# Attention and mixture-of-experts block: the products with v are given out later and in longer runs, and three small steps change place

## The chip, the cores and the metric

The kernel runs on one core of one Trainium2 chip. The metric is the device time of one execution in microseconds (us). Before the change it is 630.76 us, the median of three runs (628.73 to 631.48). Five engines work side by side, each on its own list of instructions in order: TensorE (PE, with its weight loads shown as PEld), VectorE (DVE), ScalarE (ACT), GpSimd (POOL) and SyncE (SP), which here only issues DMAs. They wait for one another through semaphores.

## The reference, cut to what matters

The input x has 8 batches of 512 tokens with 128 features. All is float32.

```python
x = x + attention(layernorm(x), Wq, Wk, Wv, Wo, bo)      # 16 heads of 8, causal
x = x + moe(layernorm(x), gate_w, w1, b1, w2, b2)        # 8 experts, the best 2 of each token

# attention, for every batch and head
s = (q * 8**-0.5) @ k.T;  s = where(causal, s, -inf)
o = softmax(s) @ v;       out = concat(o) @ Wo + bo
# experts, for every token
probs = softmax(x @ gate_w.T);  p, idx = top_k(probs, 2)
y = sum(p[j] * (relu(x @ w1[idx[j]] + b1[idx[j]]) @ w2[idx[j]] + b2[idx[j]]) for j in (0, 1))
```

## The kernel before

The work is written as seven generators (`setup`, `project`, `shifts`, `attend`, `route`, `experts`, `sums`). Each yields a planned time, in units of one batch, before each step. A loop at the end of the file (L1246) always goes on with the generator whose planned time is the least, so these numbers fix the order of the instructions on PE, ACT, DVE and SP; POOL follows its own dependences. Nothing else sorts the work: a step that yields a later number stands later in every one of these lists.

`project` normalises a batch, makes q, k and v, sends q and k through DRAM and loads them back in the layout that the score products need (L393). `shifts` makes the scores once, in `s` tiles, only to find each row's maximum (DVE `tensor_reduce`, L509); the negative maxima become two more rows of q (L463). `attend` makes the scores a second time, transposed (`st`, L644), so that ACT can turn them into exponentials (L650) in a tile `pt`, and POOL then sets to zero what lies above the diagonal (L656). Last come the products with v (L574): `va` holds v with a column of ones, and the four heads of a group write four strips of 32 partitions of one PSUM tile `po`, each product as two instructions in the profile.

A batch has four groups of four heads. The causal scores of a group come in three units (`T_UNITS`): unit 0 is key block 0 with 512 columns, unit 1 is key blocks 1 and 3 with 384 and 128 columns, unit 2 is key block 2 with 256 columns. Each unit has two steps, one for each pair of heads; after each step `go_on` (L552) is called. It gives out one waiting run of products, if there is one, and one waiting later step. A run of products is queued at the end of its unit, so it stands on PE one step after the scores that it needs. After unit 2 ACT copies `po` out (`ob`, L582), and three later steps follow: `divide` (transposes `oqp`, L592, then division on DVE), `out_T` and `out_project`. The `s` and `st` tiles share four PSUM banks (`ps_sc`); `pt` has six buffers; `po` has one.

`route` finds the experts, and 100-odd lines of small DVE operations give every token its slot; `scatter` (POOL, L913) writes the tokens to their slots in DRAM (`xs`). `dispatch` gives out tiles of 128 slots to experts. In its last part for the first seven batches, eight values are loaded into SP's registers (L892), and eight DMAs clear the rest of each expert's last tile (L900). `experts` then works tile by tile: SP loads the expert's row of `wrows` (w1, b1 and b2 side by side, L996) and gathers four tiles of tokens at a time (L1073); PE multiplies by w1 (`ph`, L1143), ACT or DVE applies bias and relu (L1150, L1152), PE multiplies by w2 (`py`, L1007), DVE adds b2 (`yo`, L1011), and `store` scatters the rows to `ys` (L1042). The row numbers for that (`to`, made by three to five small DVE operations from L1024 to L1041) are made inside `store`, at the first tile of four. From slice to slice expert tiles stand between the attention steps: steps 0 to 2 of `STEPS` (40 tiles) start during attention, 38 tiles come after it. `sums` adds the weighted outputs at the end (L1221).

`setup` fills `wrows` during the first batches. It writes all of b1 by one DMA (L260) and all of b2 by one (L263), and then w1, w2 and the cleared parts of `xs` in 28 pieces, 0.085 apart (L284).

Of the kernel before, what the change touches and what calls it, by code (L numbers as in the profile page):

```python
# [9 lines left out]
F32 = mybir.dt.float32  # L10
I32 = mybir.dt.int32
BF16 = mybir.dt.bfloat16
AF = mybir.ActivationFunctionType
ALU = mybir.AluOpType
# [10 lines left out]
def preln_attn_moe(ctx: ExitStack, tc: tile.TileContext, x, wq, wk, wv, wo, bo,  # L25
# [195 lines left out]
    def setup():  # L221
        yield -0.95
        packed_buffers(1)
        yield -0.5

        nc.gpsimd.memset(lower_bf, 1.0)
        nc.gpsimd.affine_select(
            out=lower_bf, in_=lower_bf, pattern=[[1, P]], compare_op=ALU.is_gt,
            fill=0.0, base=0, channel_multiplier=-1,
        )  # L230
        nc.gpsimd.iota(
            number, pattern=[[1, MAXT], [0, E]], base=0, channel_multiplier=0,
            allow_small_or_imprecise_dtypes=True,
        )
        for k in range(2):
            nc.gpsimd.iota(
                room[k], pattern=[[ROOM[k], E + 1]], base=0, channel_multiplier=0,
                allow_small_or_imprecise_dtypes=True,
            )

        for t, by_tile, by_row in ((place_no, P, 1), (token, 1, NT)):
            nc.gpsimd.iota(
                t, pattern=[[by_tile, t.shape[1]]], base=0, channel_multiplier=by_row,
                allow_small_or_imprecise_dtypes=True,
            )
        for e in range(E):
            nc.gpsimd.memset(rev[:, :, e : e + 1], float(E - e))
        gw_raw = const.tile([E, D], F32, tag="gwraw", name="gw_raw")
        nc.sync.dma_start(out=gw_raw, in_=gate_w)
        b1_raw = const.tile([E * FC, P], F32, tag="b1raw", name="b1_raw")  # L250
        nc.sync.dma_start(out=b1_raw, in_=b1.rearrange("e (c f) -> (e c) f", f=P))
        yield 0.4
        for dst, src, n in ((gwT, gw_raw, E), (b1T, b1_raw, E * FC)):
            pt = mm_tile(f"setup_{dst.name}")
            nc.tensor.transpose(pt[:, :n], src, ident[:n, :n])
            nc.vector.tensor_copy(
                dst if n == E else dst.rearrange("p e c -> p (e c)"), pt[:, :n]
            )
        yield 0.5
        nc.sync.dma_start(  # L260
            out=wrows[:, :, F : F + FC].rearrange("e p c -> p e c"), in_=b1T
        )
        nc.sync.dma_start(  # L263
            out=wrows[:, :, F + FC :], in_=b2.unsqueeze(1).to_broadcast([E, P, D])
        )

        pieces, after = [], []
        for e in range(E):
            after.append((wrows[e, :, 0:F], w1[e]))
            after.append((  # L270
                w2_sb.rearrange("p (c e h) -> p c e h", c=FC, e=E)[:, :, e],
                w2[e].rearrange("(c p) h -> p c h", p=P),
            ))
        for k, c0 in ((0, E * ROOM[0] // P), (1, 0)):
            n = xs[k].shape[0] // P
            for c in range(c0, n, 4):
                m = min(4, n - c)
                pieces.append((
                    xs[k].rearrange("(c p) d -> p c d", p=P)[:, c : c + m],
                    empty.unsqueeze(1).to_broadcast([P, m, XROW]),  # L280
                ))
        for n, (dst, src) in enumerate(pieces[:2] + after + pieces[2:]):
            yield 0.6 + 0.085 * n
            nc.sync.dma_start(out=dst, in_=src)  # L284


# [256 lines left out]
        indirect[0] = ins  # L543

    def attend():
        products, late, on = [], [], {}


        po = ps_o.tile([P, T], F32, tag="po", name="po")
# [2 lines left out]
        def go_on():  # L552
            ready = late[:1]
            del late[:1]
            if products:
                products.pop(0)()
            for step in ready:
                step()

# [1 line left out]
            v = u if len(unit) == 2 else 0  # L561
            return pt[:, v, at : at + W]

        def product(b, g, pts, unit, first, last):
            va = va_buf[b % 2]
            for j in sorted({j for bank in unit for _, j, _ in bank}):
                W = T - j * P
                for pr in range(2):
                    for bank in unit:
                        for u, i, at in bank:  # L570
                            if i != j:
                                continue
                            h = 2 * pr + u
                            nc.tensor.matmul(  # L574
                                po[32 * h : 32 * h + VC, j * P :],
                                lhsT=va[:, j, HG * g + h, :],
                                rhs=at_cols(pts[pr], unit, u, at, W),
                                start=(first and j == 0), stop=(last and j == 2),
                            )
            if last:  # L580
                ob = work.tile([P, T], F32, tag="ob", name=f"ob_{b}_{g}", bufs=1)
                nc.scalar.copy(ob, po)  # L582
                late.append(lambda: divide(b, ob, g))
                if g == G - 1:
                    added.add(b)
# [40 lines left out]
        for b in range(B):  # L626
            for g in range(G):
                yield b + g / G
                assert (b, g, 2) in shifted
                q2, k2 = q2_buf[b % 2], k2_buf[b % 2]  # L630
                for i, unit in enumerate(T_UNITS):
                    pts = []
                    for pr in range(2):
                        yield b + g / G + (2 * i + pr + 0.5) / 24
                        n = 2 * g + pr
                        pt = work.tile(
                            [P, 2, T], F32, tag="pt", name=f"pt_{b}_{n}_{i}", bufs=6
                        )
                        for v, bank in enumerate(unit):
                            ps = ps_sc.tile(  # L640
# [19 lines left out]
                            )  # L660
                        pts.append(pt)
                        go_on()
                    products.append(lambda b=b, g=g, pts=pts, unit=unit, i=i: product(
                        b, g, pts, unit, i == 0, i == 2))
                attended.add((b, g))
        t = B
        while products or late:
# [141 lines left out]
    def dispatch(s, soon):  # L809
# [76 lines left out]
        if k == 0 and last:  # L886

            fill = small.tile([1, E], I32, tag="fill", name=f"fill_{s}", bufs=1)
            V.tensor_tensor(fill, pc[0:1, :E], room[k][0:1, :E], ALU.add)
            yield soon()  # L890
            found = [
                nc.values_load(  # L892
                    fill[0:1, e : e + 1], engines=[mybir.EngineType.SP],
# [50 lines left out]
    def experts():  # L944
# [69 lines left out]

        sent = {k: [] for k in range(len(GROUPS))}

        def store(s, i):
            k, b, _, last = STEPS[s]
            first, m = quad(s, i)
            if i == first:  # L1020

                x = xg[s, first]
                other = small.tile([P, 4], F32, tag="other", name=f"other_{s}_{i}")
                V.tensor_tensor(  # L1024
                    other[:, :m], x[:, :m, D], slot_no[s][:, first : first + m],
                    ALU.not_equal,
                )
                goal = small.tile([P, 4], F32, tag="goal", name=f"goal_{s}_{i}")
                V.scalar_tensor_tensor(  # L1029
                    goal[:, :m], other[:, :m], float(NTOK), x[:, :m, D + 1],  # L1030
                    ALU.mult, ALU.add,
                )
                if last:
                    gap = small.tile([P, 4], F32, tag="gap", name=f"gap_{s}_{i}")
                    V.scalar_tensor_tensor(
                        gap[:, :m], x[:, :m, D], 0.0, place_no[:, first : first + m],
                        ALU.is_lt, ALU.mult,
                    )
                    V.tensor_tensor(goal[:, :m], goal[:, :m], gap[:, :m], ALU.add)  # L1039
                to[s, first] = small.tile([P, 4], I32, tag="to", name=f"to_{s}_{i}", bufs=3)  # L1040
                V.tensor_copy(to[s, first][:, :m], goal[:, :m])  # L1041
            ins = nc.gpsimd.indirect_dma_start(  # L1042
                out=ys[k],
                out_offset=bass.IndirectOffsetOnAxis(
                    ap=to[s, first][:, i - first : i - first + 1], axis=0
                ),
                in_=yo[s, first][:, i - first, :], in_offset=None,
            )
            in_order(ins)
            for other in sent[k]:  # L1050
                tc.declare_no_dep(
                    ins.ins, other, reason="every slot has its own row, or one nobody reads"
                )
            sent[k].append(ins.ins)
            if last and i == STEPS[s][2] - 1:
                tiled[k] = sent[k]
# [65 lines left out]
        def turns():  # L1122
            for s, i in quads:
                yield when(s, i + 1) - min(0.05, 1.3 * TILES_AT[s][1])
                turned[s, i] = transposed(s, i)

        yield when(0, 0)
        fetch_to(3)
# [3 lines left out]
        for n, (s, i) in enumerate(tiles):  # L1132
            first, m = quad(s, i)
            yield when(s, i + 1)
            if after(s, i):
                ph = ps_sc.tile([P, T], F32, tag="sc", name=f"ph_{s}_{i}")
                hT = work.tile([P, 2, T], F32, tag="pt", name=f"hT_{s}_{i}", bufs=6)
                hT = hT[:, 0, :].rearrange("p (c t) -> p c t", c=FC)
            else:
                ph = mm_tile(f"ph_{s}_{i}")  # L1140
# [139 lines left out]
```

## Time and profile before

| | |
|---|---|
| median of the runs | 630.76 us |
| profiled execution: its own time | 627.79 us |
| profiled execution: its span, first to last instruction | 626.0 us |
| PE busy | 555.2 us, 89% |
| DVE busy | 435.0 us, 69% |
| ACT busy | 305.3 us |
| POOL busy | 286.1 us |
| mean granted TensorE clock | 0.955 |
| products with v (L574) | 1024 instructions, 107.1 us busy |
| scores for the maximum (L486) and second scores (L644) | 117.1 and 107.4 us |

All of this is from one execution, taken by the hardware profiler. A row of the groups gives the line in the kernel, the engine, the operation, what is written and read, how often, and then the busy time, the mean of one and the idle time of the engine before it. The ends of matmuls are modelled; their starts are measured. So the cost of a run of products is read here as the time from its first start to the start of the next PE instruction. Starts and windows are in us from the first instruction.

### The profile page before, as it was taken

To read this page: it belongs to the slowest core of one execution; us is meant where nothing else is said; L and a number is where in the kernel's file an instruction comes from. 1 tells how busy PE (TensorE), PEld (TensorE's weight loads), DVE (VectorE), ACT (ScalarE), POOL (GpSimd) and SP (SyncE) were. 2 spreads that over 40 slices of the span, in tenths; PEclk is the share of its full clock that TensorE was granted. 3 is DMA by queue.
4 is the path that set the end of the run, shared out by engine and by line. 5 is a ranking of instruction groups with operands and counts; after the bars stand their busy time and mean duration, and the time that the engine had idled before them with its cause. 6 is when DMAs were issued, how large, how long until landed. Compare 5 with 4: busy or idle time off the path is not lost. (4 is left out here: it accounts for less than half of the span.)

```text
span 626.0 us, 13451 instructions
## 1 busy us (share of the span) xinstructions
PE 555.2 (89%) x4356; PEld 361.9 (58%) x4356; DVE 435.0 (69%) x1410; ACT 305.3 (49%) x679; POOL 286.1 (46%) x468
## 2 busy tenths in 40 slices
PE   8799299999989999998989999899989698999980
PEld 6544144544544554555554666566646568999980
DVE  4476366889889888686978786579785225633584
ACT  3135056566546656454654655355545344455530
POOL 3123033434636544473564355635733553676441
PEclk9889689999999999998998999899998899999995
DMA  2714816825863742470265236522321468888783
GB/s 74 179 44 119 161 25 170 201 71 157 210 110 111 170 125 89 100 175 26 81 146 127 66 120 152 151 74 65 94 70 52 121 208 258 228 269 254 245 288 98
DMA packets 66713, 85.83 MB, mean 137 GB/s; under 512 B 10652, under 2 KB 49732, under 8 KB 65636
## 3 DMA queue, kind: packets, MB, share of 16 engines
q1 hardware_dynamic: 61252, 74.90, 45.4%
q0 software_dynamic: 4544, 9.38, 4.6%
q10 hardware_dynamic: 848, 0.69, 0.4%
q8 instruction: 36, 0.59, 0.4%
q14 instruction: 33, 0.27, 0.1%
HBM read 61.14 MB, written 26.09 MB: 139 GB/s over the span
## 5 line engine op out<-in xcount | busy, mean ns | idle before, releaser
L509 DVE TENSOR_REDUCE pm<-s 128x1 f32<-128x512 f32 (+2 forms) x320 | 206.9, 682 | 69.0 <-PE s L496 68.9
L650 ACT ACTIVATE pt<-st 128x512 f32<-128x512 f32 x320 | 178.0, 599 | 105.2 <-PE st L644 96.5
L656 POOL TENSOR_SCALAR_AFFINE_SELECT pt<-pt 128x256 f32<-128x256 f32 x256 | 102.0, 411 | 208.5 <-ACT pt L650 200.6
L486 PE MATMUL s<-k,q 72*128 72x512 bf16 (+3 forms) x512 | 117.1, 308 | 20.1 <-DMA k<-kparts 13.9
L644 PE MATMUL st<-q,k 74*128 74x384 bf16 (+3 forms) x512 | 107.4, 306 | 4.0 <-DVE pm L509 2.1
L574 PE MATMUL po<-pt,va 128*9 128x512 f32 (+3 forms) x1024 | 107.1, 448 | 3.4 <-POOL pt L656 3.3
L1042 POOL DMA_INDIRECT ys<-yo,to x78 | 75.8, 972 | 54.7 <-DVE x L1221 13.1
L486 PEld LDWEIGHTS <-q 72*128 72x128 bf16 x512 | 46.9, 100 | 75.8 <-issue 60.2
L1007 PE MATMUL py<-w_sb,hT 128*128 x624 | 85.0, 279 | 2.3 <-ACT hT L1150 0.9
L496 PE MATMUL s<-mask_bf,ident_bf 128*128 128x256 bf16 (+1 forms) x320 | 82.4, 257 | 0.0
L1007 PEld LDWEIGHTS py<-w_sb,hT 128*128 128x128 f32 x624 | 76.8, 193 | 6.6 <-issue 2.5
L913 POOL DMA_INDIRECT xs<-xn_f,slot x64 | 62.8, 981 | 15.6 <-issue 13.2
L644 PEld LDWEIGHTS <-k 74*128 74x128 bf16 x512 | 46.0, 101 | 27.1 <-issue 13.6
L574 PEld LDWEIGHTS po<-pt,va 128*9 128x9 f32 x1024 | 23.7, 90 | 60.2 <-issue 31.8
L1143 PE MATMUL ph<-xgT,wt 128*128 128x128 f32 x288 | 42.6, 294 | 6.9 <-DMA wt<-wrows 6.9
L1143 PEld LDWEIGHTS ph<-xgT,wt 128*128 128x128 f32 x288 | 37.4, 203 | 11.8 <-issue 6.2
L496 PEld LDWEIGHTS <-ident_bf 128*128 128x128 bf16 x320 | 31.7, 99 | 2.2 <-issue 0.8
L1150 ACT ACTIVATE hT<-ph,q 128x128 f32<-128x128 f32 x72 | 21.2, 366 | 21.8 <-PE ph L1143 17.1
L1152 DVE TENSOR_SCALAR hT<-ph,wt 128x128 f32<-128x128 f32 x72 | 20.2, 341 | 16.3 <-PE ph L1143 16.0
L457 ACT COPY nmT<-nmTp 32x128 bf16<-32x128 bf16 x32 | 8.1, 254 | 46.2 <-PE nmTp L453 46.0
L1150 ACT ACTIVATE hT<-ph,wt 128x128 f32<-128x128 f32 x72 | 20.6, 368 | 15.4 <-PE ph L1143 9.1
L1221 DVE SCALAR_TENSOR_TENSOR x<-q,gate,x 128x128 f32<-128x128 f32 x64 | 21.4, 348 | 7.7 <-DMA q<-ys 6.6
(161 smaller groups left out, 670.7 us busy)
## 6 DMA issues: line engine op xcount, KB each, us to landing
wt<-wrows SPq DMA_DIRECT2D x36, 322.0 KB
q<-qparts SPq DMA_DIRECT2D x21, 384.0 KB
k<-kparts SPq DMA_DIRECT2D x21, 384.0 KB
q<-wrows SPq DMA_DIRECT2D x24, 322.0 KB
k<-wrows SPq DMA_DIRECT2D x18, 322.0 KB
q<-ys SPq DMA_DIRECT2D x15, 256.0 KB
k<-xs SPq DMA_DIRECT2D x42, 65.0 KB
qparts<-part SPq DMA_DIRECT2D x7, 384.0 KB
```

The lines of the kernel that those rows point to most:

```text
L486: nc.tensor.matmul(ps[:, at : at + (t + 1) * P], lhsT=q2[:KS, 2 * n + u, ts(t, P)], rhs=k2[:KS, 2 * n + u, : (t + 1) * P], start=(at == 0) ...
L496: nc.tensor.matmul(dst, lhsT=ident_bf, rhs=mask_bf if i > 0 else mask_bf[:, 0, :], start=False, stop=True, skip_group_check=True,)
L509: nc.vector.tensor_reduce(top, src, AX.X, ALU.max)
L574: nc.tensor.matmul(po[32 * h : 32 * h + VC, j * P :], lhsT=va[:, j, HG * g + h, :], rhs=at_cols(pts[pr], unit, u, at, W), start=(first and ...
L644: nc.tensor.matmul(ps[:, at : at + T - j * P], lhsT=k2[: KS + 2, 2 * n + u, ts(j, P)], rhs=q2[: KS + 2, 2 * n + u, j * P :], start=(at == ...
L650: nc.scalar.activation(pt[:, v, :], ps, AF.Exp, scale=SCALE)
L656: selects[0] = nc.gpsimd.affine_select(out=d, in_=d, pattern=[[0, 2], [1, P]], compare_op=ALU.is_ge, fill=0.0, base=0, channel_multiplier=-1,)
L913: ins = nc.gpsimd.indirect_dma_start(out=xs[k], out_offset=bass.IndirectOffsetOnAxis(ap=slot[b][:, j * NT + i : j * NT + i + 1], axis=0), ...
L1007: nc.tensor.matmul(py, lhsT=hT[:, c, :], rhs=w2_sb[:, bass.ds(at[s, i] + c * E * D, D)], start=(c == 0), stop=(c == FC - 1),)
L1042: ins = nc.gpsimd.indirect_dma_start(out=ys[k], out_offset=bass.IndirectOffsetOnAxis(ap=to[s, first][:, i - first : i - first + 1], axis=0 ...
L1143: nc.tensor.matmul(ph[:, ts(c, P)], lhsT=wt[s, i][:, ts(c, P)], rhs=turned[s, first][:, ts(i - first, P)], start=True, stop=True,)
L1150: nc.scalar.activation(hT[:, c, :], ph[:, ts(c, P)], AF.Relu, bias=bias)
```

## The change

It has five parts, all in how the work is ordered and cut:

1. `go_on` counts its calls, and a queued run of products is given out only at the second call after it was queued, not at the first. Unit 0 is still a run of its own. Units 1 and 2 are queued together after unit 2, as one run; within it the order of the key blocks stays.
2. `pt` (and `hT`, which shares its buffers after the last batch) has 8 buffers instead of 6.
3. In `setup`, b1 and b2 are written per expert, among the pieces of w1 and w2, instead of by two DMAs ahead of them; the pieces stand 0.055 apart instead of 0.085. The cleared parts of `xs` are written with consecutive rows on a partition.
4. In `dispatch`, the step that loads the eight SP registers yields eight of its small steps later instead of one.
5. The row numbers for `store` are made by a new function `goals`, which is called once for four tiles, shortly after the first of them has been multiplied by w1.

```diff
-        yield 0.5
-        nc.sync.dma_start(out=wrows[:, :, F : F + FC].rearrange("e p c -> p e c"), in_=b1T)
-        nc.sync.dma_start(out=wrows[:, :, F + FC :], in_=b2.unsqueeze(1).to_broadcast([E, P, D]))
...
             after.append((wrows[e, :, 0:F], w1[e]))
+            after.append((wrows[e, :, F : F + FC], b1T[:, e]))
+            after.append((wrows[e, :, F + FC :], b2[e].partition_broadcast(P)))
...
-                    xs[k].rearrange("(c p) d -> p c d", p=P)[:, c : c + m],
+                    xs[k][c * P : (c + m) * P].rearrange("(p c) d -> p c d", c=m),
...
-            yield 0.6 + 0.085 * n
+            yield 0.6 + 0.055 * n
...
-        products, late, on = [], [], {}
+        products, late, on, gone = [], [], {}, [0]
...
-            if products:
-                products.pop(0)()
+            gone[0] += 1
+            if products and products[0][0] + 1 < gone[0]:
+                products.pop(0)[1]()
...
-        def product(b, g, pts, unit, first, last):
+        def product(b, g, units, last):
             va = va_buf[b % 2]
-            for j in sorted({j for bank in unit for _, j, _ in bank}):
+            parts = sorted({
+                (n, j) for n, (_, unit) in enumerate(units) for bank in unit for _, j, _ in bank
+            })
+            for n, j in parts:
                 W = T - j * P
+                pts, unit = units[n]
...
-                                start=(first and j == 0), stop=(last and j == 2),
+                                start=(j == 0), stop=(j == 2),
...
-                            [P, 2, T], F32, tag="pt", name=f"pt_{b}_{n}_{i}", bufs=6
+                            [P, 2, T], F32, tag="pt", name=f"pt_{b}_{n}_{i}", bufs=8
...
-                    products.append(lambda b=b, g=g, pts=pts, unit=unit, i=i: product(
-                        b, g, pts, unit, i == 0, i == 2))
+                    units.append((pts, unit))
+                    if i != 1:
+                        products.append((gone[0], lambda b=b, g=g, units=units, i=i: product(
+                            b, g, units, i == 2)))
+                        units = []
...
             V.tensor_tensor(fill, pc[0:1, :E], room[k][0:1, :E], ALU.add)
-            yield soon()
+            yield soon(8)
...
+        def goals(s, i):
...
         def store(s, i):
             k, b, _, last = STEPS[s]
             first, m = quad(s, i)
-            if i == first:
...
                 turned[s, i] = transposed(s, i)
+                yield when(s, i + 1) + 0.3 * TILES_AT[s][1]
+                goals(s, i)
```

The body of `goals` is what stood under `if i == first:` in `store`, word for word:

```python
        def goals(s, i):
            last = STEPS[s][3]
            first, m = quad(s, i)
            x = xg[s, first]
            other = small.tile([P, 4], F32, tag="other", name=f"other_{s}_{i}")
            V.tensor_tensor(
                other[:, :m], x[:, :m, D], slot_no[s][:, first : first + m], ALU.not_equal,
            )
            goal = small.tile([P, 4], F32, tag="goal", name=f"goal_{s}_{i}")
            V.scalar_tensor_tensor(
                goal[:, :m], other[:, :m], float(NTOK), x[:, :m, D + 1], ALU.mult, ALU.add,
            )
            if last:
                gap = small.tile([P, 4], F32, tag="gap", name=f"gap_{s}_{i}")
                V.scalar_tensor_tensor(
                    gap[:, :m], x[:, :m, D], 0.0, place_no[:, first : first + m],
                    ALU.is_lt, ALU.mult,
                )
                V.tensor_tensor(goal[:, :m], goal[:, :m], gap[:, :m], ALU.add)
            to[s, first] = small.tile([P, 4], I32, tag="to", name=f"to_{s}_{i}", bufs=3)
            V.tensor_copy(to[s, first][:, :m], goal[:, :m])
```

## The prediction

> **What bounds the kernel now.** First the page: the busy times, then the slices of 15.65 us each.
>
> ```profile
> PE 555.2 (89%) x4356; PEld 361.9 (58%) x4356; DVE 435.0 (69%) x1410; ACT 305.3 (49%) x679; POOL 286.1 (46%) x468
> ...
> PE   8799299999989999998989999899989698999980
> ...
> DVE  4476366889889888686978786579785225633584
> ...
> PEclk9889689999999999998998999899998899999995
> ```
>
> PE is full nearly everywhere from slice 6 on, DVE is at 8 or 9 tenths in slices 7 to 15 and mostly lower later. So PE is the engine to free, with DVE close behind in the first half. But a busy PE may be waiting inside a run, so I read next the waits of PE (whole span), then those of its weight loads (window 80 to 512).
>
> ```profile
> PE s L486 <- DMA k<-kparts: 13.9, 2, 11.1
> PE ph L1143 <- DMA wt<-wrows: 6.9, 2, 4.3
> PE po L574 <- POOL pt L656: 3.3, 8, 1.2
> ```
>
> ```profile
> PEld po L574 <- POOL pt L656: 22.7, 52, 1.7
> PEld oqp L592 <- ACT ob L582: 14.1, 22, 1.5
> ```
>
> The columns are total, number and longest. The reader is to see that POOL's zeroing of `pt` holds up the products by 3.3 us by PE's own row, but by 22.7 us by the row of the weight loads, which stand ahead of each product and carry the semaphore. The timeline of PE settles which is real; here three runs, each with the instruction after it.
>
> ```profile
> 148.55 1.76 PE L574 MATMUL po<-pt,va 128*9 128x384 f32 x16
> 150.24 0.39 PE L486 MATMUL s<-k,q 72*128 72x512 bf16 x1
> ...
> 205.18 0.62 PE L574 MATMUL po<-pt,va 128*9 128x256 f32 x8
> 205.73 0.39 PE L486 MATMUL s<-k,q 72*128 72x256 bf16 x2
> ...
> 213.27 1.05 PE L574 MATMUL po<-pt,va 128*9 128x384 f32 x16
> 214.25 0.39 PE L486 MATMUL s<-k,q 72*128 72x512 bf16 x1
> ```
>
> The same unit 1 costs 0.98 us from start to start at 213.27 and 1.69 at 148.55: the stall is hidden in the busy time. Two more places matter. The first is the waits of SP (`SPq L892 <- DVE fill L889`, 8.4 us) and the timeline around 490:
>
> ```profile
> 489.50 4.01 SPq L900 DMA_DIRECT2D xs<-empty  x8
> ...
> 493.78 0.35 SPq L996 DMA_DIRECT2D wt<-wrows  x1
> ...
> 497.62 2.05 PE L1143 MATMUL ph<-xgT,wt 128*128 128x128 f32 x8 [4.26 <-DMA wt<-wrows]
> ```
>
> SP sits in front of the register loads, then loads eight values and clears eight tiles before it may fetch the next expert row; PE waits 4.26 us for that row. The second is the long stall of the first row of the waits, and the clock after it, from the windows:
>
> ```profile
> 74.71 0.58 PE L486 MATMUL s<-k,q 72*128 72x512 bf16 x1 [11.10 <-DMA k<-kparts]
> ```
>
> ```profile
> 78.10:84.30 6.20, 5.84 (x27) 3.12 (x27) 3.25 (x9) 2.83 (x5) 1.81 (x3) 0.50 0.28 61
> ```
>
> **Part 1, products later and in one run.** No instruction is added or removed. Unit 2's run has half of unit 1's columns (256 against 384+128) and costs 0.55 against 0.98, so 0.43 per 256 columns and about 0.125 per run whatever its length. One run fewer per group saves 0.125 us. I took all runs from the timeline in this way, in the 29 groups from 84.7 (first run of unit 0 at full clock) to 501.5: what they cost above 0.98, 0.98 and 0.55 sums to 20.2 us, in line with the 22.7 of the weight loads. The merge is worth 29 x 0.125 = 3.6. Upper bound: 23.8 us. In the new order unit 0's run follows one more step of scores and unit 2's part two more, so POOL's 0.41 us per zeroing, and the exponentials ahead of it (0.60 per bank), are done by then.
>
> How much of it stays? What is late next is the four shared banks: PE, arriving sooner, waits for DVE's maximum (0.68 per bank) or ACT's exponential. In 10 of the 29 groups (those from 119 to 197 but the one at 156, and at 234, 276, 309 and 353) DVE's busy time is already above what PE's instructions need without stalls (for instance 11.8 against 10.5 us in the group at 131.9, which takes 13.2). They hold 9.85 + 1.25 = 11.1 us of the bound; the other 19 hold 12.7. I take 40% of the first and 80% of the second: 4.4 + 10.2 = **14.6 us saved** (bounds 0 to 23.8, a loss being the rival below). The wait of `oqp` for `ob` (14.1 us at the weight loads, 7.4 of it seen in PE's starts) should shrink too, since `oqp` now stands a full step behind the run; this helps the 80%. Eight `pt` buffers cost nothing: six are alive when unit 0 of the next group is made, and the run frees four.
>
> What this part costs: in the first batch the run of unit 1 at 59.84 lies ahead of the 11.1 us stall, where it is free. It now comes after the stall, in the run at 78.33, and at half clock its 0.86 us of columns become 1.7. Here a rule speaks. The Trainium skill, "TensorE: Matmul & The Clock Gate", Part 1, says that about 3.4 us of sustained work bring the full clock back; work resumes at 74.71, so by the rule the clock is full at 78.1 and the price is 0.86. The row above has 0.50 from 78.1 to 84.3, so the measurement decides: 1.7. Against it stands part of the 0.99 us between the score starts at 79.92 and 80.91, where PE waits for DVE and then for `ob`. I take **1.0 us lost** (0 to 1.8); by the rule it would be 0.2.
>
> **Part 4, the late registers.** SP passes from the row fetched at 477.81 to the rows of tiles 5 and 6 and the gather between them before the register loads. That gather waited at 494.7 to 496.6 for the clearing DMAs, which now come after it. So the 4.26 us stall goes. With it go the half clock of 497.4 to 500.8 (the windows give 0.51, with 3.2 us of PE work in it: 1.6 us). Together 5.9. The loads (about 2.6 us) and the clearings (4.0) now stand ahead of tile 7's row, but `fill` still comes at 486.6 or earlier, so that row is issued by 494 and needed near 500. Next late is POOL, which between 480 and 515 is busy 20.3 of 35 us with scatters among the zeroings, while PE waits up to 1.67 for it. I take **4.0 us** (0 to 5.9).
>
> **Part 5, row numbers early.** Five DVE operations take 0.73 us (601.61 to 602.34, and again 610.66 to 611.39). From 598.75 to 614 DVE sets the end. The first set moves ahead of 598, where DVE waits for `ys` anyway; the second moves to about 600, inside the same stretch, and gains nothing. **0.7 us** (0 to 1.5).
>
> **Part 3, small pieces.** Two issues leave SP (0.51 and 7.01 us, the second behind a full ring at 62 to 69) and sixteen come, one of 128 rows taking about 0.55 by the w1 pieces: 8.8 us of SP, spread over 94 to about 175 us, where SP waits for `nmT` most of the time. A rule speaks against it: "DMA: Bandwidth & Descriptors", Bandwidth, has transfers under 64 KB as bound by descriptors, and eight of these are 2 KB. By it the splitting should cost several us of transfer time; in this trace the 1024 pieces of 16 bytes took about 10 ns each and their number is the same in both kernels. Queued behind are the `q<-nmT` rows, of which the first goes out at 91.8 for scores near 105; two issues ahead of it delay it by 1.1 us. The `k<-kparts` transfers that end the 11.1 us stall were issued before the two DMAs. **0** (from 0.3 gained to 2 lost).
>
> **Sum.** -14.6 + 1.0 - 4.0 - 0.7 + 0 = -18.3. The profiled execution took 627.8 us (span 626.0 and 1.8 around it): 609.5. The median of the runs is 3.0 above that execution: 630.8 - 18.3 = **612.5 us**.
>
> **Rivals.** *The banks take most of it back.* If PE, freed from POOL, waits for `ps_sc` in all groups and only a third of 23.8 stays: -7.9 + 1.0 - 2.0 = -8.9, 622. For it: DVE busy 85 and 89% of the windows 130 to 180 and 180 to 230. Against it: DVE itself waits 42.7 us for `s` in the same window. *All of it stays:* -23.8 - 5.9 - 1.0 = -30.7, 600; the groups with DVE above PE speak against it. *No effect:* the runs wait for POOL as before because POOL's chain, not PE's order, is what is late; 631. POOL's 167 us of waiting for ACT and its 46% load speak against it. *Slower: the long run starves DVE.* Between the last `s` bank before a run and the first one after it DVE has at most two maxima, 1.36 us. Before, unit 1's gap was 213.11 to 214.70, 1.6 us. Now it is two scores (0.45), the run of 1.41 and the next `s` (0.45): 2.3, so 0.7 us more DVE idle per group. If DVE sets the pace in all 30 groups and no stall is won: +21 + 1.0 - 4.7 = +17, 648. It decides from 6 groups on if the products gain nothing, and from 26 on if they gain 14.6. Against it: DVE has the small operations of `route` between the maxima, and unit 1's own gap is gone.
>
> **From these to the numbers.** Forecast 0.58 (606 to 620), a third stays 0.19, all stays 0.06, no effect 0.06, slower 0.11. A change of less than 0.5% can't be told from none here. Faster (below 627.6) is 0.83, within 0.5% 0.06, slower 0.11. The range runs to the other cases on both sides, 602 to 627.
>
> **What would show it.** Right: the weight loads' wait for `pt` falls below 6 us; merged runs of 24 take about 1.41 us; the wait of `ph` for `wt` loses its 4.3 us entry and the half clock near 497; the 11.1 us stall stays, followed by a run near 2.7 us. Wrong: waits of `s` and `st` for DVE or ACT grow by as much as those of `po` shrink, `pm` waits for `s` longer, or a new wait for `wt` stands at tile 7.

## The result: slower, because TensorE's clock fell

The changed kernel takes 639.01 us, the median of 4 runs (638.07 to 651.0), beside 629.75 for the kernel before in the same comparison: a ratio of 1.014, interval 1.010 to 1.018. The forecast was 612.5 with a range of 602 to 627. The ratios here and below leave out executions more than 1.5% slower than the fastest of their kernel (here one of four); as the clock is what this change moves, that can hide a part of its effect, so the medians of all executions are given too.

The profiled execution took 638.66 us, its span is 637.0 (before: 626.0), its mean granted clock 0.911 (before: 0.955). The page of the changed kernel, busy times and slices:

```profile
PE 554.2 (87%) x4356; PEld 369.2 (58%) x4356; DVE 431.4 (68%) x1410; ACT 307.4 (48%) x679; POOL 284.8 (45%) x468
...
PE   8798299897988899898998999989996998999980
...
PEclk9989579968878789989699999989998999999996
```

PE's busy time is what it was, 554 against 555 us, though the stalls inside the runs of products are gone. The last row shows why: from slice 8 to 19 the clock stands at 6 to 8 tenths in most places, where before it stood at 9. Next the waits between 80 and 512 us, first those of the kernel before that were not shown ahead of the prediction, then those after:

```profile
DVE pm L509 <- PE s L496: 42.7, 59, 1.9
...
PE s L486 <- ACT pt L650: 4.5, 10, 0.5
...
PE nmTp L453 <- DVE nh L524: 3.1, 2, 1.6
PE xnTp_f L313 <- DVE xn_f L304: 2.1, 3, 1.0
PE s L486 <- DVE pm L509: 1.4, 4, 0.6
```

```profile
DVE pm L504 <- PE s L491: 75.9, 49, 4.5
...
PE nmTp L448 <- DVE nh L519: 9.2, 10, 1.6
...
PE s L481 <- ACT pt L651: 7.7, 15, 0.7
PE s L481 <- DVE pm L504: 7.2, 11, 2.1
...
PEld po L574 <- POOL pt L657: 6.5, 16, 0.8
...
PE xnTp_f L308 <- DVE xn_f L299: 4.2, 6, 1.3
```

The weight loads' wait for `pt` fell from 22.7 to 6.5 us. But four waits of PE for DVE and ACT grew, together from 11.1 to 28.3 us. The timeline of PE then shows three merged runs: the first after the long stall, one in the middle of attention, both at half clock, and one at full clock.

```profile
75.57 0.59 PE L481 MATMUL s<-k,q 72*128 72x512 bf16 x1 [13.20 <-DMA k<-kparts]
...
81.20 2.75 PE L574 MATMUL po<-pt,va 128*9 128x384 f32 x24
83.88 0.61 PE L481 MATMUL s<-k,q 72*128 72x512 bf16 x1
...
132.41 2.75 PE L574 MATMUL po<-pt,va 128*9 128x384 f32 x24
135.10 0.61 PE L481 MATMUL s<-k,q 72*128 72x512 bf16 x1
...
264.70 1.48 PE L574 MATMUL po<-pt,va 128*9 128x384 f32 x24
266.12 0.39 PE L481 MATMUL s<-k,q 72*128 72x512 bf16 x1
```

From start to start a merged run costs 1.42 us at full clock and 2.68 at half clock. Between 84 and 515 us PE is at half clock for 77.3 us, before for 20.8.

**The difference as a sum.** PE is busy in 74.3 of those 77.3 us (before: 19.0 of 20.8); half of the busy time is what the half clock costs, so 37.2 against 9.5: +27.7. The products' busy time fell from 107.1 to 96.1; of these 2.0 and 14.1 us are owed to half clock and stand in the first term already, so 105.1 fell to 82.0: 23.1 us of stalls and run overhead are gone. The four waits of PE add 17.2. The stall of `oqp` for `ob`, of which 7.4 us were visible before, is gone; the wait of `ph` for `wt` fell by 3.4, PE's own wait for `pt` by 2.7; the long stalls for `k` grew by 1.5. Sum: 27.7 - 23.1 + 17.2 - 7.4 - 3.4 - 2.7 + 1.5 = +9.8. The span grew by 11.0; the other 1.2 us have no row that I could name.

### The profile page after: what moved, and what is told of

Its sections match the earlier page's. It is cut to its first block, busy times and chain, and to the rows that moved or that the text cites. A ratio compares the mean times of both kernels' runs of the same rounds, so it can differ in the third digit from the quotient of the medians.

```text
span 637.0 us, 13476 instructions
## 1 busy us (share of the span) xinstructions
PE 554.2 (87%) x4356; PEld 369.2 (58%) x4356; DVE 431.4 (68%) x1410; ACT 307.4 (48%) x679; POOL 284.8 (45%) x468
## 5 line engine op out<-in xcount | busy, mean ns | idle before, releaser
L481 PE MATMUL s<-k,q 72*128 72x512 bf16 (+3 forms) x512 | 122.3, 317 | 31.7 <-DMA k<-kparts 15.4
L645 PE MATMUL st<-q,k 74*128 74x384 bf16 (+3 forms) x512 | 112.1, 318 | 3.4 <-ACT pt L651 1.7
L481 PEld LDWEIGHTS <-q 72*128 72x128 bf16 x512 | 50.1, 101 | 99.5 <-issue 83.1
L574 PE MATMUL po<-pt,va 128*9 128x512 f32 (+3 forms) x1024 | 96.1, 502 | 0.0
L491 PE MATMUL s<-mask_bf,ident_bf 128*128 128x256 bf16 (+1 forms) x320 | 84.7, 265 | 0.0
L645 PEld LDWEIGHTS <-k 74*128 74x128 bf16 x512 | 47.3, 104 | 27.2 <-issue 14.4
L582 ACT COPY ob<-po 128x512 f32<-128x512 f32 x32 | 18.7, 585 | 34.3 <-PE po L574 34.3
```

Source lines behind the costliest of these rows:

```text
L481: nc.tensor.matmul(ps[:, at : at + (t + 1) * P], lhsT=q2[:KS, 2 * n + u, ts(t, P)], rhs=k2[:KS, 2 * n + u, : (t + 1) * P], start=(at == 0) ...
L491: nc.tensor.matmul(dst, lhsT=ident_bf, rhs=mask_bf if i > 0 else mask_bf[:, 0, :], start=False, stop=True, skip_group_check=True,)
L574: nc.tensor.matmul(po[32 * h : 32 * h + VC, j * P :], lhsT=va[:, j, HG * g + h, :], rhs=at_cols(pts[pr], unit, u, at, W), start=(j == 0), ...
L645: nc.tensor.matmul(ps[:, at : at + T - j * P], lhsT=k2[: KS + 2, 2 * n + u, ts(j, P)], rhs=q2[: KS + 2, 2 * n + u, j * P :], start=(at == ...
```

## When the clock falls

In these traces the half clock comes and goes in steps of 3.41 us: every stretch that begins between 84 and 515 us is one to five of them, always on one grid. The answer for windows on that grid, changed kernel, around one fall (length, then busy time and instructions of PE, PEld, DVE, ACT and POOL, then the granted clock, the DMA share and GB/s):

```profile
120.40:123.80 3.40, 3.32 (x30) 1.70 (x28) 3.33 (x10) 2.34 (x5) 1.75 (x3) 1.00 0.73 195
123.80:127.20 3.40, 2.18 (x17) 1.33 (x16) 3.26 (x13) 1.45 (x3) 2.16 (x5) 1.00 0.47 141
127.20:130.60 3.40, 3.40 (x16) 2.35 (x14) 3.05 (x8) 1.57 (x3) 0.65 (x2) 0.50 0.33 94
130.60:134.00 3.40, 3.40 (x23) 1.55 (x27) 0.75 (x3) 1.09 (x2) 1.83 (x3) 0.50 0.59 139
134.00:137.40 3.40, 3.40 (x26) 1.72 (x19) 1.52 (x4) 0.75 (x2) 0.00 (x0) 0.50 0.02 3
137.40:140.90 3.50, 3.50 (x28) 1.80 (x26) 2.49 (x10) 2.60 (x7) 0.77 (x2) 0.99 0.00 0
```

In the second window PE works 2.18 of 3.40 us and no run of products starts in it (the one that starts at 122.68 ends as it begins, the next is at 132.41). In the third the clock is halved, and stays so for 10.2 us although PE has no gap at all. The longest gap in the second window is 1.0 us.

I sorted all windows of this grid between 84 and 515 us that are at full clock by two marks: does PE wait for more than 18% of it, and do at least four products with v start in it? The number counted is windows, and how many of them were followed by half clock. The 18% was chosen with these traces in view.

| kernel | PE waits under 18% | waits more, with products | waits more, without |
|---|---|---|---|
| before | 107, none | 8, none | 6, of which 5 |
| after | 81, none | 6, none | 17, of which 12 |
| after, on another chip (the control in the third set below) | 75, none | 5, of which 1 | 20, of which 11 |
| merged, but at once (second experiment) | 84, none | 5, of which 1 | 19, of which 11 |

In these four traces a window of scores with some waiting is followed by half clock about two times in three (39 of 62), a window with waiting and products in 2 of 24, and one without much waiting never. The ten other traces of this case bear out a part of this. Without much waiting it is never again (none of 1026). But in the four of them that have no useless work (described below), it is 10 of 21 without products and 8 of 40 with them; and in all fourteen traces together each of the 21 windows in which PE waits for half or more was followed by half clock, four of them with products. So the waiting weighs first; products make a fall rarer at medium waiting (30 to 50%: 34 of 60 without, 6 of 20 with) but do not prevent it. In the kernel before three runs of products per group, about 4 us apart, left 6 such windows. The change leaves four of the six steps of a group without products, and 17 such windows. In 12 of the 13 ends of a half-clock stretch in the changed kernel, a run of products stood in its last window (in the kernel before in 2 of the 5 that begin after 84 us). This is a count over traces. The next runs test whether the clock is what costs; whether it falls because the products stand further apart, or because PE's waits have grown and bunched, they do not separate.

## The experiments

Each set ran on a chip of its own, beside the kernel before, whose median there was 627.49, 639.37 and 642.12 us. On the latter two the part after attention is 8 to 14 us longer in each kernel profiled there (from the last `pp` to the end 117.8 to 123.5 us, before it was 110.0). So times of different sets are not compared, only ratios, and with care the stage between the first and last `pp`: this too differed by some 8 us for one kernel in two sets (the changed kernel 414.6 and 422.3, with nine useless products 398.7 and 406.5).

### First set: which part costs, and is it the clock?

**The other parts alone.** Parts 3 to 5 of the change are kept; the products and the six buffers are those of the kernel before.

```diff
...
-            gone[0] += 1
-            if products and products[0][0] + 1 < gone[0]:
-                products.pop(0)[1]()
+            if products:
+                products.pop(0)()
...
-                    if i != 1:
-                        products.append((gone[0], lambda ...: product(b, g, units, i == 2)))
+                    products.append(lambda ...: product(b, g, pts, unit, i == 0, i == 2))
```

> Parts 3 to 5 alone (small pieces, late registers, early row numbers); products with v as in the kernel before, six buffers. Both theories (clock: the products in fewer, longer runs leave windows of 3.4 us in which the clock gate sees too little work; starvation: the long run leaves DVE without scores) put the whole loss into the products, so both expect 0.5 to 1% faster than before: 624 to 627 us, half clock between 84 and 515 us about 20 us as before (75 us in the changed kernel), no wait of 4.3 us of ph for wt. If the loss sits in the other parts (more DMA issues in SP's queue, registers late), this run is slower than before, 635 us or more.

Measured: 618.62 us (616.49 to 622.71), ratio 0.9885 (0.9775 to 0.9995); half clock 20.5 us as before, and a little faster than expected. So the loss lies in parts 1 and 2, the products and their buffers; without them the change is a gain. The eight buffers are in every run below with moved products and were not tried alone.

**Merged, but at once.** The run of units 1 and 2 is kept, the delay is not.

```diff
-            if products and products[0][0] + 1 < gone[0]:
+            if products:
```

> The changed kernel without the delay: unit 0's run and the merged run of units 1 and 2 are given out at the first call after they are queued. Clock theory: the spacing is as uneven as in the changed kernel (4 of 6 steps without a product), so half clock stays at 60 us or more and the time is 635 us or more, with waits for POOL back at unit 0. If lateness hurts and merging does not: 620 to 628 us.

Measured: 639.22 us (634.17 to 641.09), ratio 1.018 (1.007 to 1.030), half clock 64.9 us. The merging, without the delay, is enough for the whole loss.

**Later, but three runs.** The delay is kept, each unit is a run of its own.

```diff
...
-                    if i != 1:
-                        products.append((gone[0], lambda ...: product(b, g, units, i == 2)))
+                    products.append((gone[0], lambda ...: product(b, g, [(pts, unit)], i == 0, i == 2)))
```

> The changed kernel, but every unit is its own run again (8, 16, 8 instructions), still given out one step later. Clock theory: a run falls into nearly every window of 3.4 us again, half clock falls from 75 to under 35 us, and since the waits for POOL stay gone, 612 to 624 us, faster than before. Starvation theory: no run is longer than 1 us, so DVE gets its scores: also faster than before, but the half clock need not fall. If being later is what hurts: no better than the changed kernel, about 639 us.

Measured: median of 20 executions 629.8 us, but from 617.84 to 639.41; the ratio, which rests on the six quickest, is 0.990 (0.986 to 0.995), that of the medians 1.004: the usual execution is no faster than the kernel before. The program is the same in all 20; what differs is the clock. Against the mean granted clock of each execution the time falls on a line of -588 us per 1.0 of clock (correlation -0.965), from 0.944 with 617.8 us to 0.907 with 639.4. That is about what the lost clock alone would make: above, 77.3 us of half clock cost 37.2, 0.48 each, and each lowers the mean of a span of 630 us by 0.5/630, so -605 per 1.0, an estimate. The kernel before, 39 executions on that chip, has a median clock of 0.952, this one 0.919. So the delay too lowers the clock, less surely than the merging: in the profile the half clock is 52.5 us. The products stand in as many runs as before, yet PE's four waits are 23.0 us in place of 11.1. Carried on to 0.954, the clock of the other parts alone and beyond any of the 20, the line gives 611, some 8 us below their 618.6: about that much the delay is worth at equal clock, an estimate.

**Useless work.** The changed kernel whole, with nine products of zeros per group added (128 rows, 256 columns, bf16), into banks that the scores then overwrite. Nothing is left out.

```diff
                         for v, bank in enumerate(unit):
                             ps = ps_sc.tile(...)
+                            if i == 2 or (i, pr, v) == (0, 0, 0):
+                                for _ in range(3):
+                                    nc.tensor.matmul(
+                                        ps[:, : 2 * P], lhsT=idle_bf[:, :P], rhs=idle_bf,
+                                        start=True, stop=True, skip_group_check=True,
+                                    )
```

> The changed kernel plus work that nobody needs: 3 matmuls of 128x128 by 256 columns on zeros (bf16, 0.107 us each at full clock) in front of both second scores of unit 2 and of the first of unit 0, so 9 per group, 288 in all, 31 us of PE at full clock, written to a score bank ahead of the scores that overwrite it. Clock theory: half clock between 84 and 515 falls from 75 us to under 40 us, and the time changes little, 630 to 645 us, though 31 us of PE work are added. Starvation theory: the filler makes each gap between score banks longer; DVE waits longer, the half clock stays near 75 us, and the time is 650 to 670 us.

Measured: 622.15 us (616.49 to 628.85), quicker than either theory had it; ratio 0.991 (0.988 to 0.994). 288 matmuls more, some 31 us of PE work, and the ratio to the kernel before falls from 1.014 to 0.991. The half clock is 20.5 us again. This refutes the forecast's rival that the long run starves DVE: the run is as long as in the change, and work was only added. DVE's wait for `s` is 58.9 us here, less than the 75.9 of the change but above the 42.7 of before, in a kernel that is no slower than before: DVE's waiting is not what costs.

### Second set: with the clock held, what is each part worth?

**Useless work in the kernel before.** The six lines above, put into the kernel before, nothing else; a control.

> The kernel before plus the same filler of 9 full matmuls per group, a control. Half clock there is 21 us between 84 and 515 without filler. Clock theory: little is left to win, half clock 5 to 20 us; the filler's 31 us of PE work lie partly in waits, so 622 to 645 us, no gain like the 17 us of the changed kernel. If the filler helps for another reason (spacing of the scores, say), it gains here as much, 612 us or less.

Measured: 649.68 us, above the 622 to 645 expected, on a slower chip; ratio 1.017 (1.012 to 1.023). Half clock is 17.1 us. So where the clock was in order, the work costs some 11 us, and it has no merit of its own.

**Useless work, later, three runs.** The changed kernel with the edit of "later, but three runs" and the six lines of useless work together.

> Three runs of products per group, each one step later, plus the filler of 9 full matmuls per group (128 rows, zeros, ahead of both second scores of unit 2 and the first of unit 0). Clock theory: the half clock of the three-run kernel (52 us between 84 and 515) falls to about 20, and the time to 612 to 620 us; its spread from one execution to the next (618 to 639 without filler) shrinks to under 12 us. Starvation theory: 31 us more PE work make it slower than the three-run kernel without filler, 635 us or more.

Measured: 645.71 us, ratio 1.013 (1.008 to 1.018). The clock was as expected (26.7 us of half clock), the time was not: the expectation of 612 to 620 is missed even as a ratio. Against the control of its set it is 4 us quicker, which is less than parts 3 to 5 alone should bring. Of the shortfall 3.9 us lie ahead of the first `pp` (113.4 us from the start, 109.5 in the control), where the `k` of the long stall comes at 75.8 in place of 73.2; between the first and the last `pp` it gains 7.9. That the clock is kept is thus not all; why the later products bring next to nothing here is open.

**Useless work of 72 rows.** The changed kernel with nine useless products per group, of 72 rows in place of 128, as the scores have them.

```diff
-                                        ps[:, : 2 * P], lhsT=idle_bf[:, :P], rhs=idle_bf,
+                                        ps[:, : 2 * P], lhsT=idle_bf[:KS, :P], rhs=idle_bf[:KS],
```

> As the changed kernel with filler, but each filler matmul uses 72 of the 128 rows, as the scores do; the same number, columns and duration. If the gate counts only whether PE is busy: half clock 20 us and about 622 us, as with 128 rows. If it weighs the rows in use or otherwise counts such matmuls for less: half clock stays at 50 us or more between 84 and 515, and the time is 635 to 665 us.

Measured: 645.38 us (631.75 to 653.46), ratio 0.999 (0.995 to 1.004), resting on the six quickest of 20, of the medians 1.009. In the profile, one of the quicker executions with 636.67 us, the half clock is 20.5 us, as with 128 rows. But over all executions the mean clock is 0.936 against 0.949 before, while with 128 rows it is 0.952 against 0.950 (on another chip; in the third set 0.946 against 0.944). So 72 rows hold the clock in some executions, and less well on the whole. Whether it is the rows or just the filled waits that count is not settled.

**The late registers alone**, in the kernel before:

```diff
-            yield soon()
+            yield soon(8)
```

> The kernel before with the late registers alone. By the prediction's bound of this part 4.3 us of waiting and 1.6 us of half clock go, 5.9 us; the run of parts 3 to 5 shows 6.8 us less between the last two batches, so 621 to 626 us on this chip if the kernel before has 628, and the wait of ph for wt without its 4.3 us entry. If the early row numbers or the small pieces made that gain, no change, within 1.5 us of the kernel before.

Measured: 638.49 us, ratio 0.999 (0.996 to 1.002). The wait of 4.26 us for `wt` is gone, as forecast, but PE then waits elsewhere. The timeline of this kernel, PE:

```profile
487.10 0.61 PE L574 MATMUL po<-pt,va 128*9 128x256 f32 x4
490.69 1.03 PE L574 MATMUL po<-pt,va 128*9 128x256 f32 x4 [2.98 <-POOL pt L656]
491.64 2.08 PE L1143 MATMUL ph<-xgT,wt 128*128 128x128 f32 x8
```

And ACT in the same stretch:

```profile
489.07 0.58 ACT L1106 COPY xgT<-xgTp 128x512 f32<-128x512 f32 x1 [5.33 <-remote]
```

In the middle of a run of products PE waits 2.98 us for POOL's zeroing; POOL waits for ACT's exponential, and that stands behind a copy for which ACT stood still for 5.33 us. The transposes that the copy reads began at 484.95 and end in the trace by 485.6; the row names no engine as the one that was late. The half clock sets in during this wait, at 489.47 (the `ph` after it takes 2.08 instead of 1.16 us).

### Third set: a dose, and the best version

**The changed kernel once more**, without an edit, beside the others of the set.

> The changed kernel once more, beside the others of this set. Theory of the clock: ratio to the kernel before 1.01 to 1.02, half clock between 84 and 515 us from 65 to 115 us.

Measured: 657.38 us (640.36 to 658.48, 6 executions) against 642.12, a ratio of medians of 1.024, without an interval; 91.5 us of half clock. Somewhat more than expected.

**Three useless products per group** in place of nine:

```diff
-                            if i == 2 or (i, pr, v) == (0, 0, 0):
+                            if (i, pr) == (2, 1):
```

> Only three useless products per group (ahead of the last scores of the group, 0.32 us of PE per group, about 10 us in all) instead of nine. Theory that a dose of work per 3.41 us window decides: part of the loss comes back, half clock 35 to 75 us, ratio 1.000 to 1.012. If any bit of 128-row work suffices: half clock 20 to 30 us and ratio 0.985 to 0.995, better than nine, since it costs 20 us less of PE. If so little does nothing: 1.015 to 1.03.

Measured: 646.70 us (639.2 to 659.76, 22 executions), ratio 1.003 (1.000 to 1.006), of the medians 1.007; 46.0 us of half clock. All within the ranges of the theory of a dose.

**Nine once more**, the kernel of the first set.

> The changed kernel with nine useless products per group, a second time on another chip. Theory of the clock: ratio to the kernel before 0.985 to 1.000, at least 1.5% below the changed kernel of the same set; half clock 20 to 30 us. If the first result was luck of one chip: no better than the changed kernel, 1.015 or more.

Measured: 640.84 us (632.46 to 648.68, 22 executions), ratio 0.996 (0.993 to 1.000), of the medians 0.998; 29.6 us of half clock. 2.5% below the changed kernel of the set; in the ratio to the kernel before it is 0.5% worse than in the first set.

The clock of the three kernels, none, three and nine products, in their pages:

```profile
PEclk9979589977877789997899999879986999989996
```

```profile
PEclk9889689998968899997999999999969998897995
```

```profile
PEclk9989589999969999998999999999969998999995
```

| useless products per group | half clock, 84 to 515 us | PE's four waits, 80 to 512 us | median clock of the executions | median time |
|---|---|---|---|---|
| 0 | 91.5 us | 27.2 us | 0.902 | 657.4 us |
| 3 | 46.0 us | 22.4 us | 0.924 | 646.7 us |
| 9 | 29.6 us | 15.6 us | 0.945 | 640.8 us |
| kernel before | not profiled here | not profiled here | 0.945 | 642.1 us |

Read from above, time follows clock in every step, against the amount of work. The waits fall too, in part because the useless products stand in them.

**Parts 4 and 5 alone**, the late registers and the early row numbers, in the kernel before; `goals` is the function of the change.

```diff
-            yield soon()
+            yield soon(8)
...
+                yield when(s, i + 1) + 0.3 * TILES_AT[s][1]
+                goals(s, i)
```

> The late registers and the early row numbers on the kernel before, without the small pieces and with the products as before. The three parts together gave 0.9885, the registers alone 0.9988. If the late registers need the early row numbers (POOL's scatter no longer waits): ratio 0.988 to 0.993 and no wait of PE over 2 us between 484 and 502. If the registers are worth nothing and the small pieces gave the gain: 0.996 to 1.000.

Measured: 632.25 us (629.95 to 636.61), ratio 0.985 (0.980 to 0.990), the best of all. The gain is that of the other parts together, so the small pieces are not needed for it. My reason was half wrong: a wait of PE over 2 us is still there, by the timeline of PE in this kernel:

```profile
490.62 1.03 PE L574 MATMUL po<-pt,va 128*9 128x256 f32 x4 [2.20 <-POOL pt L656]
```

One part of the gain can be seen in every trace: from the last `ph` to the end it is 20.9 to 21.3 us in the three kernels with late row numbers (before, with useless work, registers alone) and 19.5 to 20.1 in those with early ones. That is some 1.2 us. The rest lies within attention: from the first `pp` to the last it is 406.0 us before, 406.9 with the registers alone, 399.7 with both parts and 399.3 with all three. One execution each. The half clock is 20.8, 30.7, 17.1 and 20.5 us in these four, so from the registers alone to both parts the clock makes most of the difference (half of the 26.9 and 15.0 us in which PE works at half clock: 6.0 of 7.2), but from the kernel before only 2.0 of 6.3. Which wait the row numbers remove there I could not show.

## Why the prediction was wrong, step by step

**The step that failed is in part 1, "How much of it stays?".** The sum there was 4.4 + 10.2 = 14.6 us saved, with bounds of 0 and 23.8. It was made of waits alone; the clock was taken to stay as it was, and priced only where the trace already showed it, after the long stall and near 497. The sum lacks a term for the clock in the middle of attention, which measured +27.7 us. The new waits of PE were also taken too small: 23.8 - 14.6 = 9.2 us were allowed for what comes back, and PE's four waits alone measured 17.2. The lower bound of 0 was not a bound either.

The rule was at hand. I had used the Trainium skill, "TensorE: Matmul & The Clock Gate", Part 1, for the stall only. The section "A second HAM failure mode: psum-queue depth-cycling" of the same page says of a kernel with bf16 matmuls that frequent short idling between groups of them makes the clock go back and forth. That is what this trace shows: the longest gap in the window ahead of each fall is 0.5 to 2.1 us in the changed kernel, below the idle window of about 3.4 us which Part 1 names for losing the clock; by that rule the 27.7 us would be 0. And the 3.4 us of sustained work that Part 1 names for getting it back was not enough at 127.2 us, where 10.2 us of uninterrupted work passed at half clock. Here the measurement decides.

**What was right in part 1.** The stalls for POOL did go: 6.5 us of 22.7 are left ("below 6" was forecast), the merged run costs 1.42 us at full clock (1.41 forecast), 23.1 us went from the products in all, the run moved behind the long stall included (23.8 was the upper bound). What is late next was named rightly too: PE's waits for DVE and ACT grew by 17.2 us. With nine useless products they sum to 15.9 us in the first set, 4.8 above the 11.1 of before; that is the least that comes back even with the clock held. How much of part 1 stays where the clock is held can be read from the stage between the first and the last `pp`, one execution each. There the change with nine useless products takes 398.7 us and the other parts alone 399.3; the useless work itself costs 10.5 (416.5 against 406.0 in the kernel before). So the moved products win some 11 us, an estimate across sets; the ratios of the whole runs (0.9885 for the other parts, 1.017 for the useless work, 0.991 or 0.996 for all together) make it 9 or 6. With three runs the working by stages gives less: 408.6 against 416.5, and of these 7.9 us parts 3 to 5 bring 6.7 (406.0 against 399.3), which leaves 1. The line through the executions of "later, but three runs" gave 8. The forecast of 14.6 is above all of these.

**The long stall.** Forecast: 1.0 us lost, the run after it near 2.7. The run costs 2.68. But `k` also came later, at 75.57 in place of 74.71, and the first `pp` stands 3.3 us later. In the kernels without the small pieces the same `k` came between 71.0 and 77.8 us, so this is no mark of the change.

**Part 2, buffers.** Forecast 0; no run has them alone. **Part 3, small pieces.** Forecast 0. Parts 4 and 5 without them gave 0.985, with them 0.9885; the intervals overlap. Nothing speaks against 0.

**Part 4, late registers.** Forecast: 4.0 us. The stall of 4.26 is gone, and alone it brings nothing (0.999). The forecast had named POOL as what is late next and still took two thirds of the gain. **Part 5** was forecast at 0.7; at the end it measured 1.2, and with part 4 beside it, 1.5% of the whole. That the two together are worth more than the sum of forecasts (4.7 us, 0.7%) was not seen.

**The rivals.** The one with the right sign, 648 us, had the wrong mechanism: DVE's wait for `s` did grow, from 42.7 to 75.9 us, but with useless work 58.9 are left and the kernel is no slower than before. A rival "the clock falls where the products are spaced further" was missing.

## What to carry to other kernels

When matmuls are moved, add a line to the sum for the clock: list the stretches of one clock window (3.41 us here) in which PE will wait, those with only light matmuls above all, and price each at half its PE work for one to five windows. Look at the row of the granted clock first whenever PE's busy time stays the same although stalls are gone; a few useless matmuls per loop are a quick test of that cause, though not a good cure. In this kernel long runs of heavy work were not better than short ones that come more often.

## What the hardware showed that I had not expected

Adding 288 useless matmuls (31 us of PE work) took 57 us of half clock away and brought the ratio to the kernel before from 1.014 down to 0.991. The same program varied from 617.8 to 639.4 us along with its clock. Ninety-six useless matmuls, 10 us of work, did half as much by the median clock of their set (0.902, 0.924, 0.945) and three quarters by the half clock (91.5, 46.0, 29.6 us, one execution each). And PE at half clock stayed there for 10.2 us without a gap. Every one of the 21 windows in which PE waited for half or more was followed by half clock, and none of the windows with less than 18% was. What else weighs in a window, rows, type or products, these runs leave open.
